# A graph attention layer on one core: thirty of 1,566 gathered chunks fetched as single rows by ScalarE and SyncE

## The chip, the core and the metric

The kernel runs on one core of a Trainium2 chip. The core has five engines with a stream of instructions each: TensorE (PE, matrix products; PEld is its weight load), VectorE (DVE), ScalarE (ACT), GpSimd (POOL) and SyncE (SP). Sixteen DMA engines move data between HBM and SBUF. ScalarE and SyncE issue plain DMAs, GpSimd issues indirect ones, which read rows at places that stand in an index tile. The metric is the time of one execution on the device in microseconds (us), as the median of several runs.

## What is computed

One layer of graph attention over 12,500 nodes of 128 features and 200,000 edges sorted by their target `dst`, with a layer norm before and a residual behind. The reference, cut to its core:

```python
h = jnp.maximum(_layernorm(x, axis=-1), 0.0)
h = (h @ W_node.T).reshape(num_nodes, H, HD)          # 4 heads of 32
e = (edge_features @ W_edge.T).reshape(num_edges, H, HD)
h_src = h[src]
att = jnp.sum(jnp.concatenate([h_src, h[tgt], e], -1) * a, axis=-1)
att = jnp.where(att > 0, att, 0.2 * att)
m = jnp.maximum(jax.ops.segment_max(att, tgt), 0.0)
ex = jnp.exp(att - m[tgt])
denom = segment_sum(ex, tgt) + (num_edges - deg)[:, None] * jnp.exp(-m)
h_prime = segment_sum((ex / denom[tgt])[:, :, None] * h_src, tgt)
return x + h_prime.reshape(num_nodes, H * HD)
```

`h_src = h[src]` is what the change is about: for each edge one row of a table is fetched, at a place that only the data tell.

## The kernel before

**Tiling.** The edges stand in 392 groups of 512 (`GE`); a group is 4 chunks (`J`) of 128 edges, one edge to a partition. Four groups are a quad (`QG`), so there are 98 quads of 16 chunks. Up to four quads are a super, over which one softmax runs. Each quad has one, two or four ranges of target nodes ("windows"), by `CLASSES`: one range for four groups in the quads 0 to 35, two ranges (of two groups) in 36 to 74, and four ranges (of one group) from 75 on. `class_of(q)[0]` is the number of groups in one range.

**Stages.** In the first tenth of the time the node rows are normed, multiplied with the weights and written to `table` in HBM: 137 floats (548 bytes) for each node. From then on each quad passes these steps:

- `gather(q, ...)`: for each chunk one indirect DMA of GpSimd (L183) puts 128 rows of `table` into the quad's place in `ga`, a ring of eight quads (`QUADS`). A semaphore of the quad (`arrived`) counts the landings.
- `all_logits(q)`: SyncE fetches edge features (`ea`), target places (`db`) and weight windows (`pw`); VectorE compares (L656), TensorE multiplies (L686, L689). Its `open_logits` begins the gathers of quad q + 2. Its `flush` calls `add_sources` for the quad before: ScalarE waits for all gathers of that quad and copies their source terms into `U` (L733).
- `softmax(s)`: once in a super, in stages: TensorE adds the terms (L790), ScalarE and VectorE alternate (L795, L800, L803 to L872), ScalarE takes the exponentials (L870) and copies the result (L888).
- `sums(q)`: four steps, one for each group. VectorE weighs the rows and marks their targets (L1082, L1084), TensorE sums (L1115); finished ranges are divided and written out. The quad's place in the ring is then free.

**Order.** The order on each engine is written out by hand: the function `together` takes the generators in turn, one step of each. In the steady part `sums(q)` runs beside `all_logits(q + 5)`, and a step of `sums` stands ahead of the step of `all_logits`. So quad q + 7 is gathered while quad q is summed, and ScalarE's copy of L733 in that round takes quad q + 4. SyncE issues its DMAs from lists (`issue`, L596), where the addresses of weights, inputs and results come from registers: `windows` (L582) loads one, two or four of them from SBUF by one instruction for a quad of one, two or four ranges. ScalarE issues a few DMAs of its own, with fixed addresses (among them L1163, L1466 and L1490).

**Memory.** `db_all` holds the target places of two quads. From quad 10 on (`OFFSETS`) they are bytes and use only the first quarter of it; the rest lies free.

Of the kernel before, what the change touches and what calls it, by code (L numbers as in the profile page):

```python
# [9 lines left out]
F32 = mybir.dt.float32  # L10
# [4 lines left out]
OP = mybir.AluOpType  # L15
AX = mybir.AxisListType

P = 128
# [8 lines left out]
R_CNT, R_SRC, ROW = H * HW, H * HW + 1, H * HW + 5  # L27

J = 4
GE = J * P  # L30
NE = GE - 1
WIDE, NARROW = 112, 80
QG = 4
# [13 lines left out]
SQUARE = 32  # L47
TWO = 2
HELD = 3
SETS = max(NODE_T, QG * J)  # L50
PAD = 1 << 20

# [5 lines left out]
def class_of(q):  # L58

    return next(c[1:] for c in CLASSES if c[0] is None or q < c[0])  # L60
# [9 lines left out]
def kernel(  # L70
# [39 lines left out]
    nc = tc.nc  # L110
    NT = -(-(N + P) // P)
    NP = NT * P
# [8 lines left out]
    table = dram.tile([NP, ROW], F32, name="table")  # L121
# [33 lines left out]
    quads = blocks(G, QG)  # L155
    nq = len(quads)
# [7 lines left out]

    spare = consts.tile([P, 6 * SBG * H], F32, name="spare")
    ga_all = consts.tile([P, QUADS, QG, J, ROW], F32, name="ga")
    GA, GATHERED = {}, set()
    arrived = [tc.alloc_semaphore(f"rows{k}") for k in range(QUADS)]
    landings = {}

    def gather(q, rows, width, lo, hi):

        g0, m = quads[q]
        ga = GA[q] = ga_all[:, q % QUADS]
        chunks = lambda i: -(-min(E - (g0 + i) * NE + 1, GE) // P)
        for i in range(lo, hi):
            if chunks(i) < J:
                nc.vector.memset(ga[:, i, chunks(i):, :], 0.0)
        order = [(i, j) for i in range(lo, hi) for j in range(chunks(i))]
        if q >= 2 * QUADS:  # L180
            order.sort(key=lambda at: at != (hi - 1, 0))
        for i, j in order:
            came = nc.gpsimd.indirect_dma_start(  # L183
                out=ga[:, i, j, 0:width], out_offset=None, in_=rows,
                in_offset=bass.IndirectOffsetOnAxis(ap=srci[:, g0 + i, j:j + 1], axis=0))
            if q >= QUADS:
                came.then_inc(arrived[q % len(arrived)], 16)
                tc.no_tile_sem_insts.add(came.ins.name)
                tc.add_to_no_dep_group(f"rows{q}", came.ins)
                landings[q] = landings.get(q, 0) + 16  # L190
# [27 lines left out]
    with tc.manual_schedule():  # L218
# [4 lines left out]
        for m in sorted({m for _, m in supers}):  # L223
            for p in range(-(-m // 2)):
                n = min(2, m - 2 * p) * QG
                to = of_head[m, p] = consts.tile([PAIR * KH, H * m * QG], F32, name=f"of_head{m}_{p}")
# [17 lines left out]
        for _ in range(AT_ONCE):  # L244
            q, i = early.pop(0)
            gather(q, x, D, i, i + 1)
# [128 lines left out]
        db_all = stay.tile([P, 2, QG, GE], I32, name="db")  # L375
# [20 lines left out]
        with tc.tile_pool(name="node", bufs=2) as node, tc.tile_pool(  # L396
# [117 lines left out]
            for b, (t0, T) in enumerate(sets):  # L514
# [5 lines left out]
                row = node.tile([P, NODE_T, ROW], F32, name="row")  # L520
# [24 lines left out]
    with tc.tile_pool(name="work", bufs=2) as work, \  # L545
# [34 lines left out]
        def windows(of, size, w, n):  # L580
# [5 lines left out]
        as_bytes = lambda d: d.bitcast(U8)  # L586
        rows_at = lambda d, at, size, n: as_bytes(d.rearrange("n c -> (n c)"))[
            bass.ds(at, n * size)].rearrange("(n c) -> n c", c=size)
# [44 lines left out]
        def fetch_rows(s):  # L633
            g0, m = groups(s)
            dr = DR[s] = turned.tile([SBG * H, NE + 2], I32, name="dr", bufs=2)
            if finer(s) > 1:
# [4 lines left out]
            nc.sync.dma_start(dr[0:H * m, :],  # L641
                              dst_rows[g0:g0 + m, :].unsqueeze(0).to_broadcast([H, m, NE + 2]))

        def open_logits(q):
            if q == supers[of_quad[q]][0]:
                fetch_rows(of_quad[q])
            if q + 2 < nq:
                fetch(q + 2)
            AT[q] = work.tile([P, QG, GE], BF16, name="at")
# [68 lines left out]
        def add_sources(q):  # L718

            s = of_quad[q]  # L720
            g0, m = quads[q]
            s0, sm = groups(s)
            keep_logits(q)
            if s not in U:
                U[s] = turned.tile([P, J, SBG * H], F32, name="U", bufs=2)
            f = finer(s)
            u = U[s][:, 0:J // f, 0:sm * H * f].rearrange("p c (h w) -> p w c h", h=H)[
                :, (g0 - s0) * f:(g0 - s0 + m) * f]
            if q >= QUADS:
                nc.scalar.wait_ge(arrived[q % len(arrived)],  # L730
                                  sum(landings[a] for a in range(QUADS, q + 1)
                                      if a % len(arrived) == q % len(arrived)))
            taken = nc.scalar.copy(u, GA[q][:, :m].rearrange("p g (f c) r -> p (g f) c r", f=f)[  # L733
                :, :, :, R_SRC:R_SRC + H])
            if q >= QUADS:
                tc.declare_no_dep(taken.ins, group=f"rows{q}",
                                  reason="a semaphore counts the gathers of this quad")
                tc.declare_fence(taken.ins, group=f"rows{q}")
            for kept in (EA, DB, PW, AT):
                del kept[q]  # L740
# [154 lines left out]
        state = {"step": 0}  # L895

        def complete(window=True, all_due=False):

            state["step"] += 1
            division = None  # L900
            if divisions and "hold" not in state and (
                    all_due or divisions[0][-1] is None or divisions[0][-1] + 2 <= state["step"]):
                division = divisions.pop(0)
            if begun and window:
                complete_window(*begun.pop())
            if division:
                divide(*division)
# [146 lines left out]
        def sums(q):  # L1054
# [8 lines left out]
            s = of_quad[q]  # L1063
# [3 lines left out]
            k, span = class_of(q)  # L1067
# [23 lines left out]
            for i in range(m):  # L1091
                g = g0 + i
                if first_fold - 4 <= q < first_fold - 4 + FOLDS:
                    shifts(q + 4, i)
                on_gpsimd = early and (q, i) > (first_fold - 2, QG - 2)
                if (q, i) not in AHEAD:
                    weighed(nc.gpsimd if on_gpsimd else nc.vector, ga, i,
                            heads(XE[s] if on_gpsimd else ex)[:, :, :, g - s0])
                    if not early:
                        mark(q, i, hot)  # L1100
                new = i % k == 0
                if not i and not later:
                    entered()
                    settled()
                if new:
                    second = k == 2 and i > 0
                    if not second:
                        bank = ps.tile([P, 512], F32, name="acc", bufs=3)
                    acc = bank[0:1 + span, ROW:2 * ROW] if second else bank[0:1 + span, 0:ROW]
                    fc = fac if g == s0 else None  # L1110
                if later and i == m - 1:
                    entered()
                least_j = 1 if k == 1 else 0
                for j in range(least_j, J)[::-1]:
                    nc.tensor.matmul(acc, hot[:, i, j, 0:1 + span], ga[:, i, j, :],  # L1115
                                     start=new and j == J - 1 and not second,
                                     stop=k > 1 and i % k == k - 1 and j == least_j,
                                     skip_group_check=k > 1)
                if i == (2 if later else 1):
                    passed_on(fac if g0 == s0 else None)  # L1120
                    if later:
                        settled()
                if not later and i == (2 if k > 1 else 1):
                    entered()
                    if k == 1:
                        settled()
                complete(new)
                if k == 1:
                    begun.append((q, i, ga, hot, pt, acc, fc))
                if i == 2 and QUADS <= q < first_fold - 5 and of_quad[q + 1] == s:  # L1130
                    READY[q + 1] = marks(q + 1)
                    beside_rows(q + 1)
                    RESTED.add(q + 1)
                if k > 1 and i == m - 1:
                    state["pending"] = q, bank
                if QUADS <= q < first_fold - 5:
                    if i % TWO == 0 and (q, i + 1) not in AHEAD and i + 1 < m:
                        weighed(nc.vector, ga, i + 1, heads(ex)[:, :, :, g + 1 - s0])
                        mark(q, i + 1, hot)
                        AHEAD.add((q, i + 1))  # L1140
                    elif i % TWO and i + 1 < m:
                        ready(q, i + 1, ga, hot)
                    elif i + 1 == m and q + 1 in READY:
                        ready(q + 1, 0, GA[q + 1], READY[q + 1])
                issue("inputs", "results")
                yield
# [418 lines left out]
        with tc.manual_schedule():  # L1565
# [20 lines left out]
            for s, (q0, m) in enumerate(supers):  # L1586
# [17 lines left out]
                for k in range(m if s == 1 else m - 1):  # L1604
                    now, ahead = ahead[:1], ahead[1:]
                    several_sums = [sums(q0 + k)]
                    if s == len(supers) - 3:
                        held_sums = sums(q0 + k + 1)
                        several_sums.append(islice(held_sums, HELD))
                    early_marks = (marked(first_fold - 2, first_fold - 1)  # L1610
# [235 lines left out]
```

## Time and profile before

| | |
|---|---|
| runs before (3) | 1997.35, 1998.41, 1998.38 us; median 1998.38 |
| profiled execution | 1998.91 us, its span 1997.1 us |
| busy PE, PEld | 1130.1, 771.6 us |
| busy DVE, ACT, POOL | 1195.0, 318.9, 1496.7 us |
| gathers of table rows (L183) | 1494, mean 946 ns |
| gathers of input rows (L183) | 72, mean 952 ns |
| DMA packets, bytes | 167747, 229.56 MB |

How to read it: the profile is one execution, seen by the hardware profiler. The span runs from the first to the last instruction; the execution's own time is 1.8 us longer. A name such as "ACT U L733" is an engine, the tile that it writes, and the line of the kernel. Sequencer work (register loads, MOVEs, the issue of DMAs by ScalarE and SyncE, waits) is not counted as busy: it is marked by a q (ACTq, SPq) and found by its line. "Idle before" is time in which the engine did nothing just ahead of an instruction, and what is named behind it ended that idleness; "issue" there means that the profile shows nothing it waited for.

### The profile page before, as it was taken

To read this page: it belongs to the slowest core of one execution; us is meant where nothing else is said; L and a number is where in the kernel's file an instruction comes from. 1 tells how busy PE (TensorE), PEld (TensorE's weight loads), DVE (VectorE), ACT (ScalarE), POOL (GpSimd) and SP (SyncE) were. 2 spreads that over 40 slices of the span, in tenths; PEclk is the share of its full clock that TensorE was granted. 3 is DMA by queue.
4 is the path that set the end of the run, shared out by engine and by line. 5 is a ranking of instruction groups with operands and counts; after the bars stand their busy time and mean duration, and the time that the engine had idled before them with its cause. 6 is when DMAs were issued, how large, how long until landed. Compare 5 with 4: busy or idle time off the path is not lost.

```text
span 1997.1 us, 18760 instructions
## 1 busy us (share of the span) xinstructions
PE 1130.1 (57%) x5116; PEld 771.6 (39%) x5116; DVE 1195.0 (60%) x2666; ACT 318.9 (16%) x1077; POOL 1496.7 (75%) x1596
## 2 busy tenths in 40 slices
PE   6566675555464645554646455546464555365555
PEld 4444454334243333343434333434343333243344
DVE  8676886456374554563755546637555475376675
ACT  6564111001001010010010100101101011121222
POOL 7777777777777777777777777777777777777775
PEclk9788788676676776766767767667677677677777
DMA  7753754434344434344444444444443453444441
GB/s 253 208 138 95 179 131 114 99 98 109 98 110 102 119 98 106 104 109 111 113 105 121 98 112 107 110 111 112 107 117 94 106 123 97 110 108 115 106 102 43
DMA packets 167747, 229.56 MB, mean 115 GB/s; under 512 B 60827, under 2 KB 100669, under 8 KB 167638
## 3 DMA queue, kind: packets, MB, share of 16 engines
q0 software_dynamic: 50112, 109.61, 24.5%
q1 hardware_dynamic: 115824, 116.14, 20.1%
q10 hardware_dynamic: 1702, 2.59, 0.4%
q8 instruction: 41, 0.67, 0.1%
q14 instruction: 68, 0.56, 0.1%
HBM read 210.74 MB, written 17.43 MB: 114 GB/s over the span
## 4 chain that ended last, share of the span: by engine, by line
POOL 41%; DVE 24%; issue 16%; PE 7%; DMA 6%; ACT 5%; SPq 0%; ACTq 0%; POOLq 0%; DVEq 0%
POOL ga L183 41%; DMA ga<-table,srci 5%; DVE at L656 3%; PE t_ps L790 2%; DVE ga L1041 1%; DVE t_ps L865 1%; DVE t_ps L804 1%; DVE t_ps L803 1%; DVE t_ps L862 1%; PE ex_ps L882 1%; DVE hot L1024 1%; PE acc L1115 1%; DVE stats L287 1%; ACT ga L309 1%; DVE pt L949 1%
## 5 line engine op out<-in xcount | busy, mean ns | idle before, releaser
L183 POOL DMA_INDIRECT ga<-table,srci x1494 | 1413.4, 946 | 456.7 <-issue 429.4
L1115 PE MATMUL acc<-ga,hot 128*113 128x137 f32 (+1 forms) x2928 | 539.4, 343 | 77.7 <-DVE hot L1024 53.3
L1115 PEld LDWEIGHTS acc<-ga,hot 128*113 128x113 f32 (+1 forms) x2928 | 479.9, 213 | 176.6 <-issue 94.5
L949 DVE SCALAR_TENSOR_TENSOR pt<-pt,spare,acc 1x133 f32<-1x133 f32 x113 | 38.2, 338 | 522.0 <-ACT den_of L943 520.6
L689 PE MATMUL lg<-at,pw 112*96 112x512 bf16 (+2 forms) x392 | 155.5, 433 | 278.1 <-DVE at L656 265.4
L686 PE MATMUL lg<-ea,by_pair 128*96 128x512 f32 (+1 forms) x392 | 227.8, 666 | 6.4 <-ACT tg L699 6.4
L656 DVE TENSOR_TENSOR at<-const_ps,db 112x1024 bf16<-112x1024 f32 (+1 forms) x176 | 212.9, 1210 | 4.5 <-DMA db<-offset 4.5
L1082 DVE TENSOR_TENSOR ga<-ga,ex_ps 128x1056 f32<-128x1056 f32 x147 | 182.2, 1240 | 0.0
L790 PE MATMUL t_ps<-ident,U 128*64 128x128 f32 (+2 forms) x210 | 46.8, 395 | 217.5 <-ACT U L733 217.5
L733 ACT COPY U<-ga 128x64 f32<-128x64 f32 x98 | 29.0, 297 | 815.8 <-DMA ga<-table,srci 815.8
L1084 DVE TENSOR_TENSOR hot<-const_ps,slot 128x896 f32<-128x896 f32 (+1 forms) x147 | 144.2, 981 | 0.0
L790 PEld LDWEIGHTS t_ps<-ident,U 128*64 128x64 f32 (+2 forms) x210 | 36.8, 200 | 243.8 <-ACT U L733 240.1
L882 PE MATMUL ex_ps<-ident,stack 128*128 128x128 f32 x105 | 28.6, 424 | 178.2 <-DVE stack L872 166.9
L968 PEld LDWEIGHTS acc<-pt,spare 1*2 1x2 f32 x226 | 14.0, 86 | 208.8 <-issue 199.9
L689 PEld LDWEIGHTS <-pw 112*96 112x96 bf16 (+2 forms) x392 | 53.9, 137 | 100.9 <-issue 98.4
L882 PEld LDWEIGHTS ex_ps<-ident,stack 128*128 128x128 f32 x105 | 18.5, 214 | 192.1 <-ACT stack L870 192.1
L183 POOL DMA_INDIRECT ga<-in_x_dram,srci x72 | 68.6, 952 | 23.2 <-issue 19.2
L1041 DVE TENSOR_TENSOR ga<-ga,ex_ps 128x528 f32<-128x528 f32 x92 | 63.6, 693 | 36.6 <-ACT xs L888 36.5
L699 ACT COPY tg<-lg 96x512 f32<-96x512 f32 (+1 forms) x51 | 29.5, 579 | 294.0 <-PE lg L689 294.0
L913 PE MATMUL acc<-ga,hot 128*81 128x137 f32 x176 | 42.6, 330 | 54.9 <-ACT ga L921 52.9
L715 PE MATMUL t_ps<-tg,of_head 96*64 96x512 f32 (+3 forms) x96 | 71.6, 838 | 0.0
L715 PEld LDWEIGHTS t_ps<-tg,of_head 96*64 96x64 f32 (+3 forms) x96 | 11.9, 172 | 153.8 <-issue 151.6
(204 smaller groups left out, 1324.9 us busy)
## 6 DMA issues: line engine op xcount, KB each, us to landing
ea<-in_edge_t_dram SPq DMA_DIRECT2D x196, 256.0 KB
ga<-table,srci POOLq DMA_INDIRECT x1494, 2.6
db<-offset SPq DMA_DIRECT2D x53, 256.0 KB
db<-in_dst_dram SPq DMA_DIRECT2D x20, 320.0 KB
db<-offset SPq DMA_DIRECT2D x35, 160.0 KB
table<-row SPq DMA_DIRECT2D x9, 616.5 KB
xt<-in_x_dram SPq DMA_DIRECT2D x9, 576.0 KB
inputs<-in_x_dram SPq DMA_DIRECT2D x92, 56.0 KB
```

Source lines behind the costliest of these rows:

```text
L183: came = nc.gpsimd.indirect_dma_start(out=ga[:, i, j, 0:width], out_offset=None, in_=rows, in_offset=bass.IndirectOffsetOnAxis(ap=srci[:, ...
L656: nc.vector.tensor_tensor(AT[q][:span, i:i + n, :].rearrange("p g e -> p (g e)"), part_ps[:span].to_broadcast([span, n * GE]), DB[q][:span ...
L686: nc.tensor.matmul(lg, by_pair[:, begin:begin + n], ea[:, i // 2, :], start=half == 0 and i == 0, stop=False, skip_group_check=True)
L689: nc.tensor.matmul(lg, PW[q][:span, begin:begin + n], at[:span, i, :], start=False, stop=full and i == quads[q][1] - 1, skip_group_check=True)
L715: nc.tensor.matmul(TP[s][:groups(s)[1] * H], of_head[supers[s][1], p][:n], tg[:n], start=p == 0, stop=False, skip_group_check=True)
L790: nc.tensor.matmul(t_ps[:R, j * P:(j + 1) * P], u[:, j, :R], ident, start=False, stop=j == C - 1, skip_group_check=True)
L882: nc.tensor.transpose(turned_ps[:, j, :], stack[:, j * P:(j + 1) * P], ident)
L949: nc.vector.scalar_tensor_tensor(to, row(w + at), passing[:, w + at:w + at + 1], own, op0=OP.mult, op1=OP.add)
L1041: engine.tensor_tensor(val, val, weight.unsqueeze(3).to_broadcast([P, J, H, HW]), op=OP.mult)
L1082: nc.vector.tensor_tensor(val, val, weight.unsqueeze(3).to_broadcast([P, TWO * J, H, HW]), op=OP.mult)
L1084: nc.vector.tensor_tensor(hot[:, i:i + TWO, :, 1:1 + span].rearrange("p g j c -> p (g j) c"), lane_ps[:, 0:span].unsqueeze(1).to_broadcast ...
L1115: nc.tensor.matmul(acc, hot[:, i, j, 0:1 + span], ga[:, i, j, :], start=new and j == J - 1 and not second, stop=k > 1 and i % k == k - 1 a ...
```

## The change

From the sums of quad 10 on, two helpers fetch some chunks in place of GpSimd, ScalarE 9 rows and SyncE 7 rows behind each of the four steps of `sums`. ScalarE's chunks are the fourth (j = 3) of the last group of a quad, SyncE's the third (j = 2). The number of chunks is that of all steps in quads of index 10 and more whose ranges have two or four groups (65 quads, 260 steps), over the steps that one chunk takes (15 for ScalarE, 19 for SyncE): 17 and 13.

For a chunk, a helper fetches its 128 source places into one partition of the free part of `db_all`; VectorE multiplies them by the bytes of a row. Every third step loads the places of three steps (27 or 21) into registers of the engine, and each row is a DMA of its own, of 548 bytes, whose address is a register. The rows land in a buffer in the free part of `db_all` (two for each helper); a semaphore counts them. In `add_sources`, ahead of the wait for the quad's gathers, ScalarE waits for the 128 rows and copies them into the quad's place in `ga`. GpSimd's `gather` leaves these chunks out. The arithmetic is the same.

```diff
-        order = [(i, j) for i in range(lo, hi) for j in range(chunks(i))]
+        order = [(i, j) for i in range(lo, hi) for j in range(chunks(i)) if (q, i, j) not in SINGLE]
...
+        class Singles:
+            def __init__(self, engine, kind, some, j, at):
+                self.engine, self.kind, self.some, self.j = engine, kind, some, j
+                free = db_all.rearrange("p k g e -> p k (g e)")[:, :, GE * (1 + at):GE * (2 + at)]
+                self.rows = [free[:, k, 0:ROW].bitcast(F32) for k in range(2)]
+                self.places = [free[0:1, k, 2 * P:3 * P] for k in range(2)]
+                self.semaphores = [nc.alloc_semaphore(f"single{at}_{k}") for k in range(3)]
+                self.steps = -(-P // some)
+                self.step, self.first, self.count = 0, None, {}
+                self.chunks = QG * sum(class_of(q)[0] > 1 for q in range(SINGLES_FROM, nq)) // self.steps
...
+            def target(self, n):
+                return self.first + n * self.steps // QG
...
+            def scale_places(self, n):
+                if n < self.chunks:
+                    nc.vector.tensor_scalar(self.places[n % 2], self.places[n % 2], float(4 * ROW),
+                                            None, op0=OP.mult)
+            def advance(self):
+                if self.first is None:
+                    self.first = state["opened"] + -(-self.steps // QG) + 1
+                    self.fetch_places(0)
+                    self.scale_places(0)
+                n, at = divmod(self.step, self.steps)
+                self.step += 1
+                q, i, j = self.chunk(n)
+                if n >= self.chunks:
+                    return
+                if not at:
+                    assert q not in GATHERED
+                    SINGLE[q, i, j] = self, n
+                    self.fetch_places(n + 1)
+                if at == QG // 2:
+                    self.scale_places(n + 1)
+                lo = at * self.some
+                if at % 3 == 0:
+                    upto = min(lo + 3 * self.some, P)
+                    self.values = nc.values_load_multi_w_load_instructions(
+                        self.places[n % 2][:, lo:upto], engines=[self.kind], min_val=0,
+                        max_val=(NP - 1) * 4 * ROW,
+                        skip_runtime_bounds_check_because="a node's row")[1]
+                for p in range(lo, min(lo + self.some, P)):
+                    came = self.engine.dma_start(
+                        as_bytes(self.rows[n % 2][p:p + 1, :]),
+                        rows_at(table, self.values[p - at // 3 * 3 * self.some], 4 * ROW, 1))
+                    came.then_inc(self.semaphores[n % 3], 16)
...
+            def put(self, n, to):
+                assert self.count[n] == P
+                nc.scalar.wait_ge(self.semaphores[n % 3], 16 * P * (n // 3 + 1))
+                taken = nc.scalar.copy(to, self.rows[n % 2])
...
+        SINGLES = [Singles(*of, at) for at, of in enumerate([(nc.scalar, mybir.EngineType.Activation, 9, 3), (nc.sync, mybir.EngineType.SP, 7, 2)])]
...
         def open_logits(q):
+            state["opened"] = q
...
         def add_sources(q):
...
+            for (a, i, j), (of, n) in list(SINGLE.items()):
+                if a == q:
+                    of.put(n, GA[q][:, i, j, :])
+                    del SINGLE[a, i, j]
             if q >= QUADS:
                 nc.scalar.wait_ge(arrived[q % len(arrived)],
...
         def sums(q):
...
                 complete(new)
+                if q >= SINGLES_FROM:
+                    for of in SINGLES:
+                        of.advance()
```

More of the change, by code (lines that the diff above doesn't have):

```diff
@@ L49 @@
 HELD = 3
+SINGLES_FROM = 10
 SETS = max(NODE_T, QG * J)
@@ L166 @@
     ga_all = consts.tile([P, QUADS, QG, J, ROW], F32, name="ga")
-    GA, GATHERED = {}, set()
+    GA, GATHERED, SINGLE = {}, set(), {}
     arrived = [tc.alloc_semaphore(f"rows{k}") for k in range(QUADS)]
@@ L642, in fetch_rows, with chunk, fetch_places @@
                               dst_rows[g0:g0 + m, :].unsqueeze(0).to_broadcast([H, m, NE + 2]))
+        class Singles:
[10 more added lines that the diff above has]
+                return self.first + n * self.steps // QG
+            def chunk(self, n):
+                return self.target(n), QG - 1, self.j
+            def fetch_places(self, n):
+                q, i, j = self.chunk(n)
+                if n >= self.chunks:
+                    return
+                g = quads[q][0] + i
+                at = ((g // 2 * J + j) * 2 + g % 2) * P
+                self.engine.dma_start(self.places[n % 2], src[at:at + P].unsqueeze(0))
+            def scale_places(self, n):
[9 more added lines that the diff above has]
+                self.step += 1
+                q, i, j = self.chunk(n)
+                if n >= self.chunks:
+                    return
+                if not at:
[16 more added lines that the diff above has]
+                    came.then_inc(self.semaphores[n % 3], 16)
+                    tc.no_tile_sem_insts.add(came.ins.name)
+                    tc.add_to_no_dep_group(f"single{self.j}_{n}", came.ins)
+                    self.count[n] = self.count.get(n, 0) + 1
+            def put(self, n, to):
+                assert self.count[n] == P
+                nc.scalar.wait_ge(self.semaphores[n % 3], 16 * P * (n // 3 + 1))
+                taken = nc.scalar.copy(to, self.rows[n % 2])
+                tc.declare_no_dep(taken.ins, group=f"single{self.j}_{n}",
+                                  reason="a semaphore counts the rows of this chunk")
+                tc.declare_fence(taken.ins, group=f"single{self.j}_{n}")
```

## The prediction

> **What bounds the kernel now.** I read the table of engines first, then the costliest groups, then the waits, and last the timeline of ScalarE (ACT) through one softmax.
>
> ```profile
> span 1997.1 us, 18760 instructions
> ...
> PE 1130.1 (57%) x5116; PEld 771.6 (39%) x5116; DVE 1195.0 (60%) x2666; ACT 318.9 (16%) x1077; POOL 1496.7 (75%) x1596
> ...
> L183 POOL DMA_INDIRECT ga<-table,srci x1494 | 1413.4, 946 | 456.7 <-issue 429.4
> ```
>
> GpSimd (POOL) is busy for 75% of the span, but nearly all its idle time is "issue": it waits for nothing that the profile shows, and simply needs 456.7/1494 = 0.306 us between two gathers of 946 ns. One gather so costs 1.25 us, and the timeline of POOL shows just that spacing, also in the middle of the kernel.
>
> ```profile
> 942.26 0.94 POOL L183 DMA_INDIRECT ga<-table,srci  x1 [0.30 <-issue]
> 943.51 0.94 POOL L183 DMA_INDIRECT ga<-table,srci  x1 [0.30 <-issue]
> 944.76 0.94 POOL L183 DMA_INDIRECT ga<-table,srci  x1 [0.30 <-issue]
> ```
>
> A quad has 16 gathers: 20.0 us. The other engines follow this pace, as the list of waits (waiter, what it waits for, us in all, times, longest) and ScalarE's timeline show (start, duration, what, and in brackets the idle time before it and what ended that):
>
> ```profile
> ACT U L733 <- DMA ga<-table,srci: 815.8, 80, 19.4
> ...
> 946.09 0.30 ACT L733 COPY U<-ga 128x64 f32<-128x64 f32 x1 [11.47 <-DMA ga<-table,srci]
> 948.45 0.59 ACT L795 ACTIVATE low<-t_ps 64x511 f32<-64x511 f32 x1 [2.06 <-PE t_ps L790]
> 948.94 0.16 ACT L943 ACTIVATE den_of<-acc 113x8 f32<-113x8 f32 x1
> 953.10 0.58 ACT L800 COPY low<-t_ps 64x511 f32<-64x511 f32 x1 [4.00 <-DVE t_ps L798]
> 959.25 0.20 ACT L858 ACTIVATE fac<-fac 1x4 f32<-1x4 f32 x1 [5.57 <-DVE fac L857]
> 962.47 0.63 ACT L870 ACTIVATE stack<-stack 64x511 f32<-64x511 f32 x1 [3.02 <-DVE stack L869]
> 964.42 0.37 ACT L888 COPY xs<-ex_ps 128x256 f32<-128x256 f32 x1 [1.32 <-PE ex_ps L882]
> ...
> 966.04 0.31 ACT L733 COPY U<-ga 128x64 f32<-128x64 f32 x1 [0.89 <-DMA ga<-table,srci]
> ...
> 986.12 0.30 ACT L733 COPY U<-ga 128x64 f32<-128x64 f32 x1 [9.19 <-DMA ga<-table,srci]
> ...
> 1026.00 0.30 ACT L733 COPY U<-ga 128x64 f32<-128x64 f32 x1 [11.32 <-DMA ga<-table,srci]
> ```
>
> The copy of L733 opens each quad and waits for its last gather; four quads later (one super) it comes 79.9 us on. Three quads of a super leave ScalarE idle for 9 to 19 us before that copy. The fourth, which holds the softmax, has 0.89 us left: between 946 and 965 ScalarE waits five times for VectorE and TensorE, 2.06 + 4.00 + 5.57 + 3.02 + 1.32 = 16.0 us.
>
> **The change, part by part.** *Removed:* 30 gathers of 1.25 us, 37 us of POOL. ScalarE takes 260 // 15 = 17 chunks and SyncE 260 // 19 = 13 (65 quads of four steps; 15 steps of 9 rows and 19 of 7 make 128). If POOL still set the pace, the span would fall by that.
>
> *Added:* 128 rows for each chunk, and each row is three things on its sequencer: a register loaded from SBUF, a MOVE, a DMA. ScalarE and SyncE run in order, so this time stands in front of their other work. First the load: L582 loads one, two or four registers by one instruction (quads of one, two and four ranges), so three answers give its slope.
>
> ```profile
> L582 SPq TENSOR_LOAD <-base_side x22: 262/268/796, 206.3 to 530.9; - x22
> ...
> L582 SPq TENSOR_LOAD <-base_side x37: 467/481/1355, 770.6 to 1492.3; - x37
> ...
> L582 SPq TENSOR_LOAD <-base_row x13: 864/877/1037, 1570.5 to 1799.0; - x13
> ```
>
> The medians 268, 481, 877 ns (middle number) give 0.20 us for each further register. 27 in one load are then about 5.5 us; batching saves only the 0.07 us that is fixed. Now the DMAs:
>
> ```profile
> L1163 ACTq DMA_DIRECT2D rows<-in_fine_ends_dram x1: 267/267/267, 1797.0 to 1797.0; - x1
> ...
> L1466 ACTq DMA_DIRECT2D rows<-in_dst_ends_dram x1: 245/245/245, 427.0 to 427.0; - x1
> ...
> L1490 ACTq DMA_DIRECT2D rows<-in_dst_rows_dram x4: 299/334/339, 606.7 to 766.6; - x4
> ...
> L596 SPq MOVE inputs<-in_x_dram x73: 29/29/29, 769.4 to 1493.7; - x73
> L596 SPq DMA_DIRECT2D inputs<-in_x_dram x73: 318/322/343, 769.5 to 1493.8; - x73
> ```
>
> A DMA's issue hardly depends on its size: 245 and 267 ns for one row (L1466, L1163), 334 for 128 (L1490). With an address from a register it has a MOVE of 29 ns ahead, and takes 322 for 112 rows. No row shows a single row with a register address; between 0.245 and 0.322 I take 0.255, as the number of rows is the nearer likeness. SyncE's timeline gives the gap to the next instruction:
>
> ```profile
> 933.98 0.32 SPq L596 DMA_DIRECT2D pw<-side  x1
> 934.35 0.42 SPq L596 DMA_DIRECT2D ea<-in_edge_t_dram  x1
> 934.81 0.43 SPq L596 DMA_DIRECT2D db<-offset  x1
> ```
>
> pw starts at 933.98, ea at 934.35, db at 934.81: 0.04 us between the end of one and the start of the next. A row has two such gaps, behind its MOVE and behind its DMA. So 0.20 + 0.029 + 0.255 + 0.08 = **0.56 us for each row on its sequencer**. Bounds: 0.485 (no MOVE and one gap: 0.20 + 0.245 + 0.04) and 0.63 (the DMA at 0.322).
>
> *ScalarE's sum over one super:* 16 steps of 9 rows, 144 x 0.56 = 80.6 us. Its own work beside that:
>
> ```profile
> sum 80.00, PE 42.99 PEld 29.47 DVE 43.79 ACT 6.73 POOL 60.50; mean PE 10.75 PEld 7.37 DVE 10.95 ACT 1.68 POOL 15.12
> ```
>
> That is 6.7 us in the four quads from 706.4 to 786.4. The copy of an arrived chunk into its quad (30 times, like the 0.3 us of L733) adds 0.6. Of the 16.0 us of waits in the softmax, those with nine rows (5 us) in front are covered: 2.06, 4.00 and nearly all of 5.57. Behind the fourth step there are no rows, so 3.02 + 1.32 and a rest of 0.6 stay: 4.9 us. Together **92.8 us against 79.9**: ScalarE becomes the bound. In bounds, 82.0 (at 0.485) to 102.9 (at 0.63).
>
> *SyncE:* 112 x 0.56 = 62.7 us in a super, beside nine DMAs of 0.32 to 0.43 and two loads of 0.48 in a quad of two ranges (I estimate 5 us with MOVEs and gaps, 20 in a super): 83. That is over 79.9 too, but under ScalarE. Behind the rows stand its features, weights, inputs and results; features and weights are issued two quads ahead of need, so being late by less than ScalarE costs nothing more. *The new wait:* ScalarE's copy into the quad waits for a chunk's 128 rows. Behind it would stand the U copy and then the softmax; but by the order of the steps a chunk's last row is issued some 1.25 quads before that copy, against 3.0 us (median) from issue to landing for a gather, so I cost it at nothing.
>
> ```profile
> DMA to landing us min/median/max: 2.5/3.0/7.9
> ```
>
> *At no cost:* the transfers. The gathers' queue has 109.61 MB at 24.5% of 16 engines; that is 200,000 rows of 548 bytes, and 0.245 x 16 x 1997 us / 200,000 = 39 ns for each.
>
> ```profile
> q0 software_dynamic: 50112, 109.61, 24.5%
> ...
> L949 DVE SCALAR_TENSOR_TENSOR pt<-pt,spare,acc 1x133 f32<-1x133 f32 x113 | 38.2, 338 | 522.0 <-ACT den_of L943 520.6
> ```
>
> 64 rows in a quad (36 and 28) are 2.5 us even if a single DMA engine carried all. The 30 scalings of places (1x128 on VectorE, like the 338 ns of L949) are 10 us and lie in its idle 45% (43.79 of 80 busy); if uncovered they cost those 10 us.
>
> *The sum:* the rows run from the sums of quad 10 for 255 steps, 15.9 supers. 15.9 x (92.8 - 79.9) = +205 us. Quad q + 7 is gathered in the sums of quad q, where today quad q + 4 has just landed; so while ScalarE is late, POOL may come two quads further ahead. Behind quad 75 the others can catch up with it, as ScalarE is idle there before three of four L733 copies:
>
> ```profile
> 1705.77 0.30 ACT L733 COPY U<-ga 128x64 f32<-128x64 f32 x1 [10.91 <-DMA ga<-table,srci]
> ...
> 1725.99 0.30 ACT L733 COPY U<-ga 128x64 f32<-128x64 f32 x1 [12.41 <-DMA ga<-table,srci]
> ...
> 1745.64 0.30 ACT L733 COPY U<-ga 128x64 f32<-128x64 f32 x1 [13.76 <-DMA ga<-table,srci]
> ```
>
> That returns 2 x 20 = 40 us. Net +165: 1998.9 (the profiled execution's own time, 1.8 above its span and 0.5 above the median of the three runs, 1998.38) + 165 = **2164 us**. At 0.485: 15.9 x 2.1 = 33, of which the 40 leaves nothing: 1999, no change. At 0.63: 15.9 x 23.0 = 366 - 40: 2325.
>
> **The rivals.**
> *Faster: the rows fit.* ScalarE waits 815.8 us for gathers, and if a row cost under (79.9 - 12.2)/144 = 0.47 us the rows would lie in that wait, POOL would stay the bound, and 30 x 1.25 = 37 us go: 1961 us. It needs a load slope or a one-row issue well below the rows above, say 0.15 + 0.2. For it: no row shows 27 registers in one load, nor a one-row DMA by register. Against: the slope is straight over 1, 2, 4.
> The Trainium skill speaks for this rival: DMA: Bandwidth & Descriptors, section Issuing engines are not separate DMA queues, says that issuing from several engines saves sequencer time, "which is usually small relative to the DMA itself". Here the rows say otherwise: 0.245 us to issue against 39 ns to move a row.
>
> *Slower still: the two sequencers hinder each other, or ScalarE's loads are dearer.* At the start both issue at once, and ScalarE's 128-row DMA takes 0.45 against 0.334 alone.
>
> ```profile
> 1.17 0.45 ACTq L264 DMA_DIRECT2D we<-in_w_edge_dram  x1
> ...
> L1557 ACTq TENSOR_LOAD <-flag x1: 481/481/481, 1976.5 to 1976.5; - x1
> ...
> L1557 SPq TENSOR_LOAD <-flag x1: 287/287/287, 1979.6 to 1979.6; - x1
> ```
>
> 0.12 us more on each row: 144 x 0.68 + 12.2 = 110.1, and 15.9 x 30.2 - 40 = +440: 2439 us. Also ScalarE needed 481 ns for one register where SyncE needed 287; if each cost it 0.48, a row would be 0.84, a super 133, the time 2800.
> Perfetto Trace Analysis of the Trainium skill, section DMA Instruction — HWDGE (DVE, Sync), has the mechanism: one descriptor generator serves both sequencers and is locked for one of them at a time. The row of L264 is in line with it, though it is from the first microseconds.
>
> *No change:* at 0.485 to 0.49 per row the loss and the 40 us returned cancel: 1995 to 2003.
>
> **Chances.** Forecast (0.49 to 0.63 a row) 55%; faster 22%; dearer rows 15%; no change 8%. So faster by over 0.2% (4 us, about what a measurement of this kernel can tell from no change) 22%, within 8%, slower 70%. The forecast's own range is 2003 to 2325. For 8 in 10 the range must take in the faster case but not the dearest one: 1958 to 2330.
>
> **What would show it.** Right: TENSOR_LOADs of 27 registers near 5.5 us on ScalarE; DMAs of 0.25 us in rows of nine; L733 no longer waiting for gathers between 320 and 1570 us, its copies 23 us apart; POOL idle for longer than "issue", waiting for slots. Wrong: gathers still 1.25 us apart there, or loads of 27 registers under 3 us.

## The result and the profile after

The changed kernel takes 1985.87 us (median; 1980.47 to 1990.28) against 1998.38 before: ratio 0.994, 95% interval 0.9919 to 0.9961. It is faster by some 12 us, where 2164 us was forecast, and it gains a third of the 37 us that 30 gathers cost.

The profiled execution is one of 1985.87 us with a span of 1984.1. First the page's table of engines and the costliest group of GpSimd (after; the added lines moved L183 to L184 and L733 to L814):

```profile
span 1984.1 us, 26735 instructions
...
PE 1125.2 (57%) x5116; PEld 771.9 (39%) x5116; DVE 1203.4 (61%) x2696; ACT 331.0 (17%) x1107; POOL 1467.7 (74%) x1566
...
L184 POOL DMA_INDIRECT ga<-table,srci x1464 | 1384.3, 946 | 472.3 <-issue 451.3
```

The 30 gathers are gone (1494 to 1464), and one still takes 946 ns. The idle time before them rose from 456.7 to 472.3 us, though there are fewer. The list of waits of the changed kernel (waiter, what it waits for, us in all, times, longest) shows where that is:

```profile
POOL ga L184 <- issue: 468.3, 1451, 7.5
...
ACT tg L776 <- issue: 252.6, 29, 12.6
...
ACT U L814 <- issue: 188.2, 19, 15.0
...
ACT U L814 <- DMA ga<-table,srci: 103.8, 14, 14.0
```

Two things are new. GpSimd has gaps of up to 7.5 us: 468.3 - 1451 x 0.305 leaves 26 us of stall above the usual spacing (0.305 us is the idle time before a gather where nothing holds it up). And ScalarE's copy into U waits for gathers for 103.8 us, where it waited for 815.8; what stands before it and before the copy of L776 is now "issue", in which ScalarE's sequencer is at its rows (its timeline below). The stalls look so in GpSimd's timeline (after):

```profile
1336.70 0.94 POOL L184 DMA_INDIRECT ga<-table,srci  x1 [0.30 <-issue]
1337.95 0.94 POOL L184 DMA_INDIRECT ga<-table,srci  x1 [0.30 <-issue]
1346.40 0.94 POOL L184 DMA_INDIRECT ga<-table,srci  x1 [7.50 <-issue]
```

What the rows cost on their sequencers stands at their two lines (after; count, then least, median and greatest duration in ns):

```profile
L701 ACTq MOVE db<-table x2176: 29/29/38, 304.7 to 1595.7; - x198
L701 ACTq DMA_DIRECT2D db<-table x2176: 227/235/540, 304.8 to 1595.7; - x198
L701 SPq MOVE db<-table x1664: 29/29/38, 304.5 to 1569.7; - x185
L701 SPq DMA_DIRECT2D db<-table x1664: 224/228/357, 304.6 to 1569.7; - x185
```

The last line below is a batch of seven issues in ScalarE's timeline, merged into one line. It gives the spacing with MOVE and gaps: (2.19 - 0.235)/6 = 0.326 us a row, where the prediction had 0.364 (0.029 + 0.255 + 0.08).

```profile
914.96 0.56 ACTq L701 DMA_DIRECT2D db<-table  x2
915.31 0.30 ACT L814 COPY U<-ga 128x64 f32<-128x64 f32 x1
915.46 0.17 ACT L1024 ACTIVATE den_of<-acc 113x8 f32<-113x8 f32 x1
915.61 2.19 ACTq L701 DMA_DIRECT2D db<-table  x7
```

The loads are the surprise. These are ScalarE's of two stretches, the second and third of its first chunk, then the last of that chunk and the first of the next:

```profile
L696 ACTq TENSOR_LOAD <-db x2: 5934/5980/6025, 316.7 to 334.5; - x2
...
L696 ACTq TENSOR_LOAD <-db x2: 1549/1970/2391, 364.6 to 373.8; - x2
```

A chunk loads its 128 places from the values 0, 27, 54, 81 and 108 on. The three in the middle take 6.0 us for 27 registers (0.22 each), the first 2.39 us for 27 (0.09), the last 1.55 for 20 (0.08). The cheap ones begin at byte 0 and byte 432 of the list (a place has 4 bytes), both multiples of 16; the others at 108, 216 and 324, which are not. On average a chunk pays 22 us, 0.17 for a row, and a row costs 0.326 + 0.17 = **0.50 us**.

Last the pace, from the copies into U of quad 22 and quad 74, 13 supers apart. They are numbered by counting these copies from the first quad, here and below: before, then after.

```profile
466.72 0.30 ACT L733 COPY U<-ga 128x64 f32<-128x64 f32 x1 [12.65 <-DMA ga<-table,srci]
...
1505.35 0.30 ACT L733 COPY U<-ga 128x64 f32<-128x64 f32 x1 [11.50 <-DMA ga<-table,srci]
```

```profile
465.42 0.30 ACT L814 COPY U<-ga 128x64 f32<-128x64 f32 x1
...
1531.07 0.30 ACT L814 COPY U<-ga 128x64 f32<-128x64 f32 x1
```

1038.6/13 = 79.9 us a super before, 1065.7/13 = 82.0 after. So in this stretch the changed kernel is slower by 27 us; yet its span ends 13 us earlier.

### The profile page after: what moved, and what is told of

It is laid out like the page before. It is cut to its first block, busy times and chain, and to the rows that moved or that the text cites. A ratio compares the mean times of both kernels' runs of the same rounds, so it can differ in the third digit from the quotient of the medians.

```text
span 1984.1 us, 26735 instructions
## 1 busy us (share of the span) xinstructions
PE 1125.2 (57%) x5116; PEld 771.9 (39%) x5116; DVE 1203.4 (61%) x2696; ACT 331.0 (17%) x1107; POOL 1467.7 (74%) x1566
## 5 line engine op out<-in xcount | busy, mean ns | idle before, releaser
L184 POOL DMA_INDIRECT ga<-table,srci x1464 | 1384.3, 946 | 472.3 <-issue 451.3
L1196 PE MATMUL acc<-ga,hot 128*113 128x137 f32 (+1 forms) x2928 | 534.2, 341 | 101.6 <-DVE hot L1105 53.4
L1196 PEld LDWEIGHTS acc<-ga,hot 128*113 128x113 f32 (+1 forms) x2928 | 476.1, 212 | 197.6 <-issue 88.2
L763 PE MATMUL lg<-ea,by_pair 128*96 128x512 f32 (+1 forms) x392 | 241.5, 702 | 134.3 <-ACT tg L776 134.3
L733 DVE TENSOR_TENSOR at<-const_ps,db 112x1024 bf16<-112x1024 f32 (+1 forms) x176 | 213.0, 1211 | 35.9 <-DMA db<-offset 33.9
L1163 DVE TENSOR_TENSOR ga<-ga,ex_ps 128x1056 f32<-128x1056 f32 x147 | 182.1, 1239 | 0.0
L763 PEld LDWEIGHTS lg<-ea,by_pair 128*96 128x96 f32 (+1 forms) x392 | 66.0, 196 | 144.4 <-ACT tg L776 139.9
L792 PE MATMUL t_ps<-tg,of_head 96*64 96x512 f32 (+3 forms) x96 | 66.2, 779 | 76.0 <-ACT tg L776 76.0
L184 POOL DMA_INDIRECT ga<-in_x_dram,srci x72 | 68.7, 953 | 23.4 <-issue 17.1
L776 ACT COPY tg<-lg 96x512 f32<-96x512 f32 (+1 forms) x51 | 29.5, 579 | 321.4 <-issue 252.6
L814 ACT COPY U<-ga 128x64 f32<-128x64 f32 x98 | 29.0, 297 | 292.8 <-issue 188.2
L871 PE MATMUL t_ps<-ident,U 128*64 128x128 f32 (+2 forms) x210 | 43.5, 374 | 41.3 <-ACT U L814 41.3
```

Of the source, the lines that this page charges most:

```text
L184: came = nc.gpsimd.indirect_dma_start(out=ga[:, i, j, 0:width], out_offset=None, in_=rows, in_offset=bass.IndirectOffsetOnAxis(ap=srci[:, ...
L733: nc.vector.tensor_tensor(AT[q][:span, i:i + n, :].rearrange("p g e -> p (g e)"), part_ps[:span].to_broadcast([span, n * GE]), DB[q][:span ...
L763: nc.tensor.matmul(lg, by_pair[:, begin:begin + n], ea[:, i // 2, :], start=half == 0 and i == 0, stop=False, skip_group_check=True)
L792: nc.tensor.matmul(TP[s][:groups(s)[1] * H], of_head[supers[s][1], p][:n], tg[:n], start=p == 0, stop=False, skip_group_check=True)
L871: nc.tensor.matmul(t_ps[:R, j * P:(j + 1) * P], u[:, j, :R], ident, start=False, stop=j == C - 1, skip_group_check=True)
L1163: nc.vector.tensor_tensor(val, val, weight.unsqueeze(3).to_broadcast([P, TWO * J, H, HW]), op=OP.mult)
```

## The theory and the experiments

**Theory.** From quad 10 to 75 ScalarE is the bound at 82.0 us a super. GpSimd, with 30 gathers less (30 x 1.25 = 37.5 us), needs 79.9 - 37.5/15.9 = 77.5 and runs ahead by 4.5 us in each super, 71 us in 15.9 supers, until the ring of eight quads is full. It stalled 26 us, so the ring gave it room for 45; this 45 is fitted to the one run, and the runs below test it. Behind the last rows nothing hinders GpSimd, and the kernel ends with it: the time before, less 1.25 us for each gather removed, plus the stalls, 1998.4 - 37.5 + 26 = 1987. Where there is no stall, that a super lasts longer for the others costs nothing.

Two things in the trace bear this out. That the ring is what stops GpSimd shows at the places of the stalls. All eight that leave more than 0.6 us of idle time stand before the first gather of a quad (63, 65, 68, 71, 72, 75, 76 and 80, counted in the kernel's order of gathers), the first of them at 1238 us; and each ends 0.77 us behind the last matrix product (L1196) of the quad eight places before, which had the same place in the ring (a quad has 32 of these products). For the stall of 7.5 us, before quad 68, that is the end of this line, 1344.44 + 1.19 = 1345.63, against 1346.40 (after):

```profile
1344.44 1.19 PE L1196 MATMUL acc<-ga,hot 128*113 128x137 f32 x8
```

That the kernel ends with GpSimd shows at the last gathers, before and after. They end 33.7 and 33.9 us before the end of the span, so what stands behind them has not changed:

```profile
1962.48 0.94 POOL L183 DMA_INDIRECT ga<-table,srci  x1 [0.30 <-issue]
...
1949.29 0.94 POOL L184 DMA_INDIRECT ga<-table,srci  x1 [0.30 <-issue]
```

**Rivals.** SyncE is the bound, not ScalarE. Or the row DMAs hinder each other or the gathers, by the issue of both engines or by their traffic. Or each row does a little harm in its place.

**ScalarE alone.**

```diff
-        SINGLES = [... [(nc.scalar, mybir.EngineType.Activation, 9, 3), (nc.sync, mybir.EngineType.SP, 7, 2)])]
+        SINGLES = [... [(nc.scalar, mybir.EngineType.Activation, 9, 3)])]
```

> ScalarE's 17 chunks alone; SyncE fetches no rows, GpSimd takes its 13 chunks back. Theory: between quad 10 and 75 ScalarE is the bound (82 us a super), GpSimd runs ahead until the ring of eight is full and then stalls. GpSimd saves 17 x 1.25 = 21 us; the stall is 15.9 x (82.0 - 78.6) - 46 = 8 us; time 1986, a super still about 82 us, ScalarE's copy into U seldom waiting for a gather. Rival, SyncE is the bound: a super falls to 78.6 us, no stalls, 1977.

Measured 1982.09 us, ratio 0.9919 (0.9905 to 0.9932). The copies of quad 22 and 74 in this run:

```profile
465.73 0.30 ACT L814 COPY U<-ga 128x64 f32<-128x64 f32 x1
...
1527.65 0.30 ACT L814 COPY U<-ga 128x64 f32<-128x64 f32 x1
```

1061.9/13 = 81.7 us a super: with no row on SyncE the pace of the full change is all but kept, so ScalarE sets it. The time lies between the two expected ones. GpSimd's list of waits shows a stall of 454.1 - 1479 x 0.305 = 3 us (with a longest of 1.2) where 8 were expected; that is a part of why the time is under 1986:

```profile
POOL ga L184 <- issue: 454.1, 1479, 1.2
```

And the issue of a row on ScalarE takes as long without SyncE's rows as with them, 234 ns against 235 (lines of L701 in this run):

```profile
L701 ACTq DMA_DIRECT2D db<-table x2176: 227/234/647, 304.9 to 1591.9; - x198
```

**SyncE alone.**

```diff
-        SINGLES = [... [(nc.scalar, mybir.EngineType.Activation, 9, 3), (nc.sync, mybir.EngineType.SP, 7, 2)])]
+        SINGLES = [... [(nc.sync, mybir.EngineType.SP, 7, 2)])]
```

> SyncE's 13 chunks alone. Theory: SyncE has about 5 us of slack in a super, GpSimd stays the bound at 78.9 us a super, no stalls in the window, the full 13 x 1.25 = 16 us are gained: 1982, faster than all 30 chunks together. Rival, SyncE is the bound: a super stays near 82 us, GpSimd stalls, 1986 or more.

Measured 1980.54 us, ratio 0.9918 (0.9905 to 0.9932): 16.7 us less than the 1997.26 of before beside it, for 13 x 1.25 = 16.3. Copies of quad 22 and 74:

```profile
465.12 0.30 ACT L814 COPY U<-ga 128x64 f32<-128x64 f32 x1 [13.55 <-DMA ga<-table,srci]
...
1489.68 0.30 ACT L814 COPY U<-ga 128x64 f32<-128x64 f32 x1 [11.69 <-DMA ga<-table,srci]
```

78.8 us a super, and the copies wait for gathers again: GpSimd is the bound, SyncE is not. Thirteen chunks gain more than the thirty of the change did (16.7 us against 12.5, each by medians).

**Half the stretch.** `SINGLES_FROM = 10` becomes `SINGLES_FROM = 42`, nothing else.

> Both helpers begin at quad 42 instead of 10: 8 + 6 = 14 chunks, each step as long as before. Theory (ring): 8.2 supers x (82.0 - 77.8) = 35 us that GpSimd gains on ScalarE, less than the 46 us for which the ring has room: no stalls, the full 14 x 1.25 = 17.5 us, 1981, better than 30 chunks. Rival, each row harms in its place: 14/30 of the 12.5 us that the change gained, 1992.

Measured 1981.13 us, ratio 0.992 (0.9907 to 0.9934), as the theory with the ring has it. GpSimd has no stall (longest 0.3 us), though ScalarE is as loaded as in the full change while it lasts (81.5 us a super from quad 50 to 74, against 82.3 there in the change):

```profile
POOL ga L184 <- issue: 445.8, 1462, 0.3
```

**Fewer rows in a step.** 9 and 7 become 6 and 5.

> The change's own loads (three steps at a time), but 6 rows by ScalarE and 5 by SyncE behind a step: 11 + 10 = 21 chunks. Theory: ScalarE needs about 60 us a super, GpSimd stays the bound at 78.2, no stalls, the full 21 x 1.25 = 26 us: 1971, so fewer chunks gain more than the change's 30. Rival, the gain goes with the number of rows: 21/30 of 12.5 us, 1988.

Measured 1971.92 us, ratio 0.9877 (0.9862 to 0.9892): 25.3 us gained with 21 chunks, of the 26.2 that their gathers cost. GpSimd has no stall:

```profile
POOL ga L184 <- issue: 445.6, 1461, 0.3
```

**Loads that begin at multiples of 16 bytes.**

```diff
-                if at % 3 == 0:
-                    upto = min(lo + 3 * self.some, P)
-                    self.values = nc.values_load_multi_w_load_instructions(
-                        self.places[n % 2][:, lo:upto], engines=[self.kind], min_val=0,
...
                 for p in range(lo, min(lo + self.some, P)):
+                    if p % 24 == 0:
+                        self.values = nc.values_load_multi_w_load_instructions(
+                            self.places[n % 2][:, p:min(p + 24, P)], engines=[self.kind], min_val=0,
...
-                        rows_at(table, self.values[p - at // 3 * 3 * self.some], 4 * ROW, 1))
+                        rows_at(table, self.values[p % 24], 4 * ROW, 1))
```

> All 30 chunks, the same rows, but registers are loaded 24 at a time, at places that are multiples of 24 values, so every load begins at a multiple of 16 bytes. In the changed kernel loads that begin there took 0.07 to 0.09 us for a register, the others 0.20 to 0.22. Theory: a load of 24 takes 1.7 us, ScalarE's super falls from 82 to about 72 us, GpSimd is the bound again, all 37 us are gained: 1961. Rival, the row DMAs themselves hold things up (issue of both engines, or their traffic): loads get shorter but the time stays near 1986. Rival, SyncE is the bound: it has the same gain here, so also 1961; the run with one engine alone decides that.

Measured 1961.4 us, ratio 0.9821 (0.9808 to 0.9835). The same 3840 rows, the same issue of 235 and 228 ns; only the loads differ:

```profile
L696 ACTq TENSOR_LOAD <-db x102: 823/1775/1956, 302.6 to 1526.8; - x102
L696 SPq TENSOR_LOAD <-db x78: 750/1682/1932, 303.1 to 1495.6; - x78
```

```profile
463.30 0.30 ACT L813 COPY U<-ga 128x64 f32<-128x64 f32 x1 [3.80 <-DMA ga<-table,srci]
...
1472.21 0.30 ACT L813 COPY U<-ga 128x64 f32<-128x64 f32 x1 [6.20 <-DMA ga<-table,srci]
```

24 registers take 1.78 us, 0.074 each, and a super takes 1008.9/13 = 77.6 us, GpSimd's 77.5. The copies wait for gathers again, GpSimd has no stall, and 35.9 of the 37.5 us are there. That speaks against every rival that blames the row DMAs: they are all still issued.

```profile
POOL ga L184 <- issue: 447.1, 1465, 0.5
```

**The same loads, 4 bytes further on.** The only edit on the kernel above:

```diff
-                self.places = [free[0:1, k, 2 * P:3 * P] for k in range(2)]
+                self.places = [free[0:1, k, 2 * P + 1:3 * P + 1] for k in range(2)]
```

> The loads of 24 again, 9 and 7 rows, 30 chunks; only the places stand 4 bytes further on in SBUF, so that no load begins at a multiple of 16 bytes. Theory: a load of 24 takes 5.3 us in place of 1.8, ScalarE needs 137 x (0.32 + 0.22) + 7 + 9 = 90 us a super against GpSimd's 77.5, the stall is 15.9 x 12.5 - 45 = 154 us: about 2114, slower than before the change. Rival, the number of loads or their size made the difference: 1961 as without the shift.

Measured 2103.82 us, ratio 1.0538 (1.0522 to 1.0554). The lines of its loads, its GpSimd's waits, and its copies of quad 22 and 74:

```profile
L696 ACTq TENSOR_LOAD <-db x102: 2022/5430/5672, 302.9 to 1713.2; - x102
L696 SPq TENSOR_LOAD <-db x78: 1888/5132/5348, 303.8 to 1671.2; - x78
```

```profile
POOL ga L184 <- issue: 574.7, 1459, 11.5
...
POOL ga L184 <- ACT t_ps L840: 9.7, 2, 8.1
...
POOL ga L184 <- ACT ga L1132: 3.4, 3, 1.7
```

```profile
492.79 0.30 ACT L813 COPY U<-ga 128x64 f32<-128x64 f32 x1
...
1643.21 0.30 ACT L813 COPY U<-ga 128x64 f32<-128x64 f32 x1
```

Four bytes turn 1.78 us for a load into 5.43 (0.226 for a register). A super takes 1150.4/13 = 88.5 us. GpSimd stalls for 574.7 - 1459 x 0.305 = 130 us in its first line and for 12 above the usual spacing in the two others, 142 in all; beside one at 104 us, ahead of all rows, each of its longer stalls ends 0.77 us behind the quad eight places before, as in the change. The time before, less the gathers, plus the stalls, is 1997.2 - 37.5 + 142 = 2102, against 2100.84 for the profiled execution and 2103.82 for the median. The ring's formula, with the 45 of the change, gives 15.9 x (88.5 - 77.5) - 45 = 130 of these 142; why 12 are missing is open. This is how the forecast's loss looks when it does come.

**More rows, with the cheap loads.** Loads of 24 as above, and 10 and 8 rows behind a step in place of 9 and 7.

> Loads of 24 at multiples of 24 as before, and 10 rows by ScalarE, 8 by SyncE: 20 + 16 = 36 chunks. Theory: with loads of 24 ScalarE still waited some 8 us a super for gathers; 20 rows more a super at 0.40 us use that up: about 78 us against GpSimd's 77.1, which the ring takes. All 36 x 1.25 = 45 us: 1952. Rival, there is a further limit near 30 chunks (SyncE, the row traffic): 1961 or slower.

Measured 1953.67 us, ratio 0.9784 (0.9771 to 0.9797): 36 chunks, 43.5 of the 45 us that their gathers cost, no stall. It is the fastest of all, some 32 us under the changed kernel.

```profile
POOL ga L184 <- issue: 444.1, 1456, 0.3
...
ACT U L813 <- issue: 144.4, 12, 14.3
ACT U L813 <- DMA ga<-table,srci: 128.7, 17, 13.1
```

ScalarE now waits for gathers for 128.7 us in the whole run, against 356.9 with 9 and 7: little of its idle time is left, and more rows may bring the stalls back (not tried).

## Why the prediction was wrong, point by point

**What bounds the kernel before: right.** GpSimd's 1.25 us for a gather carried every result: the five kernels without a stall gained 16.7, 16.1, 25.3, 35.9 and 43.5 us for 13, 14, 21, 30 and 36 gathers, 1.15 to 1.29 us for each.

**The row's price: 0.56 forecast, 0.50 measured.** The issue of one row takes 0.235 us where 0.255 was taken from the lines of one-row DMAs (L1466, L1163), and MOVE and gaps 0.09 where 0.11 was. The load's slope of 0.20, straight over one, two and four registers, was right for long loads only where they begin off a multiple of 16 bytes; two of five begin on one, so 0.17 came out. The loads quoted could not show that. Those of four registers begin at the places 114, 118 and so on of their list, always 8 bytes past a multiple of 16, and two registers cost the same wherever they begin. These are two loads of the kernel before, for the quads 36 and 37, at byte 144 of the list, a multiple of 16, and at byte 152:

```profile
L582 SPq TENSOR_LOAD <-base_row x1: 473/473/473, 791.7 to 791.7; - x1
...
L582 SPq TENSOR_LOAD <-base_row x1: 470/470/470, 812.6 to 812.6; - x1
```

**The number of rows: 144 a super forecast, 137 done.** The fifteenth step of a chunk of ScalarE has only two rows (128 - 14 x 9); the sum counted nine in each step. That is a mistake of counting, worth 4 us of the 92.8.

**ScalarE becomes the bound: right in kind, but 92.8 us a super forecast and 82.0 measured.** 137 x 0.50 = 68 and its own busy time of 7.4 (96.81 us in 13 supers) leave some 6 us, by difference, for waits in the softmax, where 4.9 was forecast. The line gives the stretch, its length, and the busy time (and instructions) of PE, PEld, DVE, ACT and POOL, then clock, DMA share and GB/s (after):

```profile
465.40:1531.10 1065.70, 575.51 (x2460) 391.55 (x2460) 582.55 (x1118) 96.81 (x337) 789.24 (x836) 0.70 0.44 107
```

That 82.0 is also the lower bound of the prediction, for its cheapest row, is chance: it was made of 144 rows at 0.485. Of the 178 us between 2164 and the measured time, 15.9 x 10.8 = 172 come from the super's length alone.

**The step that failed: the 40 us that come back.** At this bound the prediction wrote "15.9 x 2.1 = 33, of which the 40 leaves nothing: 1999, no change", and let the return make good the loss, no more. But the comparison was with GpSimd's old pace. The 30 gathers left GpSimd at once, whatever ScalarE did; it needs 77.5 us a super, and ends 37 us earlier unless the ring stops it. The right sum at the same 82.0 is 15.9 x 4.5 = 71 us ahead, 45 taken by the ring, 26 stalled: -37 + 26 = -11, measured -12.5 (the 45 is fitted to these 26; the runs with one engine, with half the stretch and with the shift are its tests). This is the prediction's own sum with 45 for 40 and without the cap: 33 - 40 = -7 would have had the right sign. With this formula the forecast's own 92.8 would have given 1998.9 - 37.5 + (15.9 x 15.3 - 45) = 2160, so the central value fell by the length of the super, and the sign by the cap: no change would be at 82.7 us a super, not at 82.0 (77.5 + (45 + 37.5)/15.9). The half stretch tells it best: ScalarE over its limit for 33 quads left 16.1 of 17.5 us.

**SyncE: right in its place, wrong in its size.** It carries 13 chunks and is not the bound, as forecast. But its 83 us a super, over the old 79.9, did not come: alone with its rows the kernel keeps GpSimd's pace of 78.8.

**The new wait for 128 rows, and the transfers: right.** No listed wait of the copies of the rows into the ring (L713) names a row DMA, and 4608 rows (36 chunks) came through without a stall of GpSimd.

**The rivals.** *The rows fit* was wrong as put for the change, which stayed over its threshold (0.50 against 0.47), but its time, 1961, is what came when the loads became cheap (0.074 + 0.326 = 0.40 us a row). The range for 8 in 10, 1958 to 2330, holds 1985.87 only because it was stretched down to this rival, whose mechanism is not what happened in the change. The sentence that the Trainium skill gave it, from DMA: Bandwidth & Descriptors, section Issuing engines are not separate DMA queues, that the issue is "usually small relative to the DMA itself", is no guide for such rows: 0.235 us of issue stand against the 39 ns that moving a row takes on the gathers' queue. No row here shows how long a single-row DMA takes from issue to landing. *The two sequencers hinder each other* fell: 234 ns for ScalarE's issue alone, 235 beside SyncE's rows. What Perfetto Trace Analysis of the Trainium skill says of one descriptor generator locked for one sequencer (section DMA Instruction — HWDGE (DVE, Sync)) leaves no trace in these medians. *ScalarE's loads are dearer* was true in direction only: 0.22 a register beside SyncE's 0.20 to 0.21, not 0.48.

**The signs: mixed.** Three of the four loads of 27 registers in a chunk took 6.0 us, near the 5.5 that was to prove the forecast right, and one 2.4, under the 3 that was to prove it wrong. GpSimd did wait for places in the ring, but only eight times; between them its gathers stayed 1.25 us apart.

## What to carry to other kernels

When work is taken off the pacing engine and put on another that then gets too slow, ask how far the first may run ahead: with a ring between them, a loss counts only from the point where the ring is full, measured against the pacing engine's new time, not its old. Price a sequencer's work in whole instructions, register loads and MOVEs too, for 0.5 us a row is much where thousands stand in front of an engine's own work. Lay out long lists that registers are loaded from so that each load begins at a multiple of 16 bytes.

## What the runs showed of the hardware

In loads of 20 to 27 registers from SBUF, a register costs 0.06 to 0.09 us when the load begins at a multiple of 16 bytes of its list, and 0.20 to 0.23 when it begins 4, 8 or 12 bytes past one: 1.78 against 5.43 us for 24 on ScalarE, 1.68 against 5.13 on SyncE, by a shift of 4 bytes alone. ScalarE's loads of 20, 24 and 27 registers from such a multiple take 1.55, 1.78 and 2.39 us, so the first four more cost 0.06 each and the last three 0.20 each. That, and the two registers at 0.47 us wherever they begin, would fit a low price for whole groups of four registers only; no run was made to test it. The Trainium skill (Runtime: NRT & Kernel Launch, section Instruction fetch mechanics) states some 200 ns for a register "even for bulk", for loads from HBM; from SBUF the shifted loads agree, and the others take under half.

The issue of a plain DMA of one row takes 0.235 us on ScalarE and 0.228 on SyncE, by an address in a register, and does not grow when both issue at once.

The three kernels that ScalarE's sequencer paces for all of the stretch spread more than the others: by 9.8 us over the runs of the change (1980.47 to 1990.28), 6.3 with ScalarE alone and 5.1 with the shift, against 1.8 to 2.5 in the five without a stall. Why was not examined.
